# Attention and a Mamba block on one Trainium2 core: dt projected from high and low parts in one pass, and the maxima split before their transposes

## The chip, the cores and the metric

The kernel runs on one core of a Trainium2 chip. A core has five engines that run side by side and wait for each other by semaphores: TensorE (PE, matmuls, writes PSUM), VectorE (DVE), ScalarE (ACT), GpSimd (POOL) and SyncE (SP, which here only issues DMAs). The metric is the device time of one execution in microseconds; lower is better. All times of the profile are microseconds unless they are marked ns.

## The reference

The input x is (4, 128, 64, 64): four images of 128 channels and 4096 tokens. Two layers follow one another.

```python
# layer 0: attention over the 4096 tokens of an image, 4 heads of 32
Q, K, V = (split_heads(x_flat @ Wn + bn) for n in "qkv")
attn = softmax(Q @ K.T * 32**-0.5)                 # 4096 x 4096 per head
y = (attn @ V) @ Wo + bo + x_flat
x = (y - mean(y)) / sqrt(var(y) + 1e-5) * gamma + beta
# layer 1: three terms are summed
spatial  = conv3x3(x, conv_spatial_w) + conv_spatial_b
spectral = irfft2(conv_spectral_w @ [real, imag](rfft2(x)) + conv_spectral_b)
xi, z = split(in_proj_w @ x)                       # 256 + 256 rows
xs = silu(causal_conv1d(xi, 4 taps))
x_dbl = x_proj_w @ xs                              # 8 + 16 + 16 rows: dt's rank, B, C
dt = softplus(dt_proj_w @ x_dbl[:8] + dt_proj_b)   # 256 rows
h = exp(dt * A) * h + dt * B * xs                  # scan over the tokens, 16 states
out = spatial + spectral + out_proj_w @ ((h . C + D * xs) * silu(z))
```

## The kernel before

All tensors are float32 in memory. Some tiles are of the type float32r; the code splits a value into a high part that such a tile holds and the low rest, and multiplies both.

The tokens are cut into 32 chunks of 512 (8 per image). Attention runs over 64 halves H (a chunk's 512 queries and a pair of heads), each in 32 steps, one step per 128 keys. One outer loop runs over the steps t and writes the work of all stages side by side, by hand (`tc.manual_schedule()`); each engine works its instructions off in the order in which they are written. A step holds, in this order:

- `scores_for_exp(H, m)` (lines 475 to 492): six PE matmuls into the PSUM tile s (tag s2), the last two of which add minus the row's maximum as `sel` x `MX[H]`; then ACT takes exp into e.
- `scores_for_max` (427 to 446), for half H + 1 and seven steps ahead: four PE matmuls into the other s (tag s1), of which DVE takes maxima into part.
- pieces of the scan of an earlier chunk (`scan_state`, `scan_decay`, `scan_input_term`): dA on ACT, hs on DVE, db, hs and acc on POOL, and the load of B and C rows spread over partitions (bc) by SP.
- a turn of the plan, which runs jobs.
- `times_values` for the step before: two PE matmuls po with e.

Jobs are generators in a `Plan` (100 to 152). At each `yield` a job names what it needs next: "P", "D" or "A" are places on PE, DVE or ACT in this step, "B" one of two spare PSUM banks. In attention an odd step has two places of each kind, an even step one place on ACT alone; before and after attention each step has four of each. A job whose needs aren't met waits for a later step; jobs of low rank go first. `plan.release(bank, n)` gives the bank back n steps later.

The jobs that matter here are these.

- `maxima(H)` (448 to 471) starts seven steps ahead of half H, with rank 0. It takes a bank, reduces part to mx (128 x 8: 4 tiles of 128 queries x 2 heads) on DVE, copies each value over 64 columns into wide with four POOL copies (line 455), transposes the four tiles on PE into pm (462), and makes MX: ACT writes minus the high part to mhi (469), and DVE adds the low part on those rows for which `minus_lo` is set (470). MX has the high part in rows 0 to 31 of a head's 64 and the low part in rows 32 to 63; `sel` picks one row of each kind. Of these steps only the bank is asked for; the places of DVE, PE and ACT aren't.
- `scan_bc(c)` (707 to 721) multiplies xs by x_proj (pd, 40 rows: 8 of dt, 32 of B and C), lets ACT copy pd to xd, stores the 32 rows to bcd by an SP DMA, and starts two `scan_dt`.
- `scan_dt(c, hf, xd)` (723 to 761) multiplies the 8 rows by dt_proj, with both in float32 (pdt, line 726), for 128 of the 256 rows of dt; then follow the steps of softplus on ACT, DVE and POOL.
- `gate(c)` and `convolve(c)` compete with these for places (pz at line 769, pf at lines 903 and 908).

The weights are loaded at the start by DMAs that ACT issues (190 to 241). For the last two chunks, after attention has ended, the scan's sum is made on PE (acc, line 852).

Of the kernel before, what the change touches and what calls it, by code (L numbers as in the profile page):

```python
# [9 lines left out]
F32 = mybir.dt.float32  # L10
F32R = mybir.dt.float32r
AF = mybir.ActivationFunctionType
ALU = mybir.AluOpType
# [4 lines left out]
P = 128  # L18
W = 64
HEADS = 4  # L20
HD = P // HEADS
PAIRS = HEADS // 2
HS = P // 2
L = 512
RPC = L // W
TPC = L // P
DI = 256
NH = DI // P
NS = 16
DTR = 8  # L30
# [14 lines left out]

K_ID, K_HIL, K_G = 0, P, 2 * P
K_LO = K_G + W
K_SEL = K_LO + 1
NCONST = K_SEL + P


def _constants():

    w = np.arange(W)
    k = np.arange(1, W // 2)
    sin = np.sin(2 * np.pi * np.outer(w, k) / W).sum(1) * 2 / W
    hil = sin[(w[:, None] - w[None, :]) % W]
    c = np.zeros((P, NCONST), np.float64)
    c[:, K_ID : K_ID + P] = np.eye(P)  # L70
    for r in range(2):
        s = slice(r * W, (r + 1) * W)
        c[s, K_HIL + r * W : K_HIL + (r + 1) * W] = hil.T
    c[:, K_G : K_G + W] = -sin
    for j in range(2):
        c[j * HS + HD : (j + 1) * HS, K_LO] = 1.0
        c[j * HS, K_SEL : K_SEL + P] = 1.0
        c[j * HS + HD, K_SEL : K_SEL + P] = 1.0
    return c.astype(np.float32)


# [74 lines left out]
def attention_then_conv_mamba(  # L156
# [17 lines left out]
    nc = tc.nc  # L174
    ctx.enter_context(tc.manual_schedule())
    B, C, N = x.shape
# [6 lines left out]
    const = ctx.enter_context(tc.tile_pool(name="const", bufs=1))  # L183
    att = ctx.enter_context(tc.tile_pool(name="att", bufs=2))
    loc = ctx.enter_context(tc.tile_pool(name="loc", bufs=2))
# [9 lines left out]
    for h in range(HEADS):  # L195
        k, j = divmod(h, 2)
# [3 lines left out]
    for h in range(HEADS):  # L200
        k, j = divmod(h, 2)
        c = COL["bk"] + k
# [8 lines left out]
    for h in range(HEADS):  # L211
        k, j = divmod(h, 2)
        c = COL["bq"] + h
# [17 lines left out]
    nc.scalar.dma_start(cw, conv_w)  # L231
    inw = const.tile([P, 2 * DI], F32, name="inw")
    nc.scalar.dma_start(inw, in_w)
    xpw = const.tile([P, NH, DTR + 2 * NS], F32, name="xpw")
    nc.scalar.dma_start(xpw, xp_w.rearrange("(h p) r -> p h r", p=P))
    dtw = const.tile([DTR, DI], F32, name="dtw")
    nc.scalar.dma_start(dtw, dt_w)
    outw = const.tile([P, NH, P], F32, name="outw")
    nc.scalar.dma_start(outw, out_w.rearrange("(h p) o -> p h o", p=P))
    spw = loc.tile([P, 2, 2 * P], F32, tag="sgz", name="spw", bufs=1)  # L240
# [2 lines left out]
    def col(name, k=0):  # L243
        return vec[:, COL[name] + k : COL[name] + k + 1]

    in_lo = cst[:, K_LO : K_LO + 1]
    ident = cst[:, K_ID : K_ID + P]
    hilbert = cst[:, K_HIL : K_HIL + P]
    minus_lo = const.tile([P, 1], F32, name="minus_lo")
    sel = const.tile([P, P], F32R, name="sel")  # L250
    ones = const.tile([P, 1], F32, name="ones")
    nc.vector.memset(ones, 1.0)
# [9 lines left out]

    def constants_of_attention():
        yield ""
        nc.vector.tensor_scalar(minus_lo, in_lo, -1.0, None, ALU.mult)
        nc.vector.tensor_copy(sel, sel_f)

    def constants_of_the_rest():


        yield ""
        half = loc.tile([P, 2, 2 * P], F32, tag="sg1", name="half", bufs=1)
        nc.vector.tensor_scalar(half, spw, 0.5, None, ALU.mult)
        rr, ir = half[:, 0, :P], half[:, 0, P:]
        ri, ii = half[:, 1, :P], half[:, 1, P:]
        yield ""
        g_id = loc.tile([P, P], F32, tag="ob", name="g_id", bufs=1)
        nc.gpsimd.tensor_tensor(g_id, rr, ii, ALU.add)
        nc.gpsimd.tensor_tensor(cw[:, 4, :], cw[:, 4, :], g_id, ALU.add)
        nc.gpsimd.tensor_tensor(g_flip, rr, ii, ALU.subtract)  # L280
        nc.gpsimd.tensor_tensor(g_hil, ri, ir, ALU.subtract)
        nc.gpsimd.tensor_tensor(g_fliphil, ri, ir, ALU.add)
        yield ""
        nc.vector.tensor_scalar(sbias, cst[:, K_G : K_G + W], col("spec_bi"), None, ALU.mult)
        nc.vector.tensor_tensor(sbias[:, 0:1], sbias[:, 0:1], col("spec_br"), ALU.add)

        nc.scalar.activation(negA, vec[:, COL["A_log"] : COL["A_log"] + NH * NS], AF.Exp)
        yield ""
        nc.vector.tensor_scalar(negA, negA, -1.0, None, ALU.mult)


        bank = yield "PB"
        pb = bank_tile(bank, [P, 1], "pb")
        nc.tensor.matmul(pb, Wo, bvc, start=True, stop=True)
        yield "D"
        plan.release(bank, 2)
        nc.vector.tensor_tensor(bo, pb, col("bo"), ALU.add)
# [5 lines left out]
        [const.tile([P, L], F32R, name=f"K_{k}_{i}") for i in range(NCH)] for k in range(PAIRS)  # L303
    ]
    VA = [const.tile([P, TPC, HEADS, HD + 1], F32, name=f"V_{i}") for i in range(NCH)]
    state = const.tile([P, NH * NS], F32, name="state")
    carry = const.tile([P, NH, TAPS - 1], F32, name="carry")

# [5 lines left out]
    def bank_tile(bank, shape, name):  # L314
        return psum.tile(shape, F32, tag=f"m{bank}", name=name)
# [66 lines left out]
    QT, MX = {}, {}  # L382
# [64 lines left out]

    def maxima(H):

        bank = yield "B"  # L450
        mx = att.tile([P, TPC, 2], F32, tag="mx", name=f"mx_{H}")
        nc.vector.tensor_reduce(mx, part.pop(H), AX.X, ALU.max)  # L452
        wide = att.tile([P, TPC, 2, HS], F32, tag="wide", name=f"wide_{H}", bufs=1)
        for t in range(TPC):
            nc.gpsimd.tensor_copy(  # L455
                wide[:, t], mx[:, t].unsqueeze(2).to_broadcast([P, 2, HS])
            )
        for _ in range(3):
            yield ""
        pm = bank_tile(bank, [P, L], f"pm_{H}")  # L460
        for t in range(TPC):
            nc.tensor.transpose(
                pm[:, t * P : (t + 1) * P], wide[:, t].rearrange("p j d -> p (j d)"), ident
            )
        yield ""
        plan.release(bank, 2)
        mhi = att.tile([P, L], F32R, tag="th", name=f"mhi_{H}", bufs=1)
        mm = att.tile([P, L], F32R, tag="MX", name=f"MX_{H}")
        nc.scalar.activation(mhi, pm, AF.Copy, scale=-1.0)
        nc.vector.scalar_tensor_tensor(mm, mhi, minus_lo, pm, ALU.mult, ALU.subtract)  # L470
        MX[H] = mm

    es, po, oz = {}, {}, {}

# [232 lines left out]
    def scan_bc(c):  # L707

        bank = yield "PB"
        pd = bank_tile(bank, [DTR + 2 * NS, L], f"pd_{c}")  # L710
        for hf in range(NH):
            nc.tensor.matmul(pd, xpw[:, hf, :], xss[c][hf], start=hf == 0, stop=hf == NH - 1)
        yield "A"
        plan.release(bank)
        xd = loc.tile([DTR + 2 * NS, L], F32, tag="xd", name=f"xd_{c}", bufs=1)
        nc.scalar.activation(xd, pd, AF.Copy)
        yield ""
        bcds[c] = dram.tile([2 * NS, L], F32, tag="bc_d", name=f"bcd_{c}")
        nc.sync.dma_start(bcds[c], xd[DTR:, :])
        for hf in range(NH):  # L720
            plan.now(1, scan_dt(c, hf, xd))

    def scan_dt(c, hf, xd):
        bank = yield "PB"
        pdt = bank_tile(bank, [P, L], f"pdt_{c}_{hf}")
        nc.tensor.matmul(
            pdt, dtw[:, hf * P : (hf + 1) * P], xd[:DTR, :], start=True, stop=True
        )


        yield "A"
# [417 lines left out]
```

## Time and profile before

| | before |
|---|---|
| median of 3 runs | 6135.8 us (6135.27 to 6138.95) |
| the profiled execution: time, span | 6136.61 us, 6134.7 us |
| mean granted TensorE clock | 0.986 |
| busy: PE, DVE, ACT, POOL | 96%, 70%, 58%, 74% |
| pdt (line 726): records, mean ns | 128, 639 |
| wide (line 455): copies, busy | 256, 63.1 us |
| MX (line 470): operations, mean ns | 64, 746 |
| mhi (469) and xd (716): operations, mean ns | 64, 589 and 32, 577 |

Busy time is the sum of an engine's instructions over the span. PEld is the load of TensorE's weights, which overlaps PE's matmuls. Records of matmuls overlap each other too, so the mean length of a record is longer than the distance from one start to the next. A float32 product shows as two records, a float32r product as one. In the lines of groups there stand the line of the kernel, the engine, the operation, output<-inputs, shapes and count; then busy us and the mean ns of one; then the engine's idle time just before, with what ended most of it.

### The profile page before, as it was taken

What the parts mean: (1) busy time and instruction counts of PE and PEld (TensorE: products, weight loads), DVE (VectorE), ACT (ScalarE), POOL (GpSimd) and SP (SyncE); (2) the same over time, 40 slices, a digit from 0 to 9 for tenths busy, and PEclk for the clock granted to TensorE, in tenths of its full rate; (3) what the DMA queues carried; (4) which work ended last, traced back from release to release, by engine and by line L of the source; (5) the groups of instructions that cost most, each with busy time, mean ns of one, the idle gap of its engine ahead of it and who ended that gap; (6) DMA issues with size and microseconds to landing.
All of it is one profiled execution on the core that took longest, in us unless ns stands there. A gap on an engine that the chain in (4) does not pass through costs nothing. (4 is left out here: it accounts for less than half of the span.)

```text
span 6134.7 us, 82692 instructions
## 1 busy us (share of the span) xinstructions
PE 5914.9 (96%) x31434; PEld 2454.4 (40%) x31434; DVE 4291.6 (70%) x4404; ACT 3557.2 (58%) x4794; POOL 4534.8 (74%) x4785
## 2 busy tenths in 40 slices
PE   5999999999999999999999999999999999999966
PEld 2444444444444444444444444444444444444321
DVE  4556776777776777777767777677777677777647
ACT  1455666665666665666665666666565566566643
POOL 0006888778887777888877888877888787788877
PEclk7999999999999999999999999999999999999988
DMA  4012222224322222222332322222432222222222
GB/s 126 23 35 57 75 65 73 72 69 110 89 78 74 72 70 71 73 66 84 102 89 72 74 75 65 73 72 68 111 82 75 69 65 63 65 66 69 67 82 82
DMA packets 265503, 455.21 MB, mean 74 GB/s; under 512 B 45577, under 2 KB 47121, under 8 KB 265105
## 3 DMA queue, kind: packets, MB, share of 16 engines
q1 hardware_dynamic: 261584, 448.11, 26.9%
q8 instruction: 246, 4.03, 0.3%
q10 hardware_dynamic: 3520, 1.82, 0.1%
q14 instruction: 153, 1.25, 0.1%
HBM read 375.63 MB, written 65.80 MB: 72 GB/s over the span
## 5 line engine op out<-in xcount | busy, mean ns | idle before, releaser
L446 DVE TENSOR_REDUCE part<-s 128x2 f32<-128x1024 f32 x2048 | 2497.4, 1220 | 1527.0 <-PE s L439 1526.5
L491 ACT ACTIVATE e<-s 128x1024 f32<-128x1024 f32 x2048 | 2095.3, 1023 | 2203.1 <-PE s L483 2195.7
L503 PE MATMUL po<-e,V 128*33 128x512 f32 x8192 | 2158.6, 605 | 0.7
L483 PE MATMUL s<-Q,K 64*128 64x512 f32 x8192 | 1504.0, 445 | 7.1 <-ACT e L491 3.8
L439 PE MATMUL s<-K,Q 64*128 64x512 f32 x8192 | 1314.6, 398 | 31.5 <-DVE part L446 28.5
L839 POOL TENSOR_TENSOR hs<-hs,bc 128x512 f32<-128x512 f32 x952 | 1215.7, 1277 | 174.0 <-DVE hs L829 105.4
L483 PEld LDWEIGHTS s<-Q,K 64*128 64x128 f32 x8192 | 610.9, 185 | 1727.9 <-ACT e L491 1175.1
L818 POOL TENSOR_TENSOR db<-u,bc 128x512 f32<-128x512 f32 x948 | 1215.4, 1282 | 0.0
L858 POOL TENSOR_TENSOR acc<-acc,hs 128x512 f32<-128x512 f32 x900 | 1150.8, 1279 | 70.6
L829 DVE TENSOR_TENSOR_SCAN hs<-dA,state,db 128x512 f32<-128x512 f32 x832 | 1060.2, 1274 | 106.9 <-ACT dA L813 53.1
L439 PEld LDWEIGHTS s<-K,Q 64*128 64x128 f32 x8192 | 762.0, 185 | 255.2 <-DVE part L446 77.1
L483 PE MATMUL s<-MX,sel 64*128 64x512 f32 x4096 | 813.4, 394 | 25.9 <-DVE MX L470 25.9
L813 ACT ACTIVATE dA<-dt,negA 128x512 f32<-128x512 f32 x1024 | 703.1, 687 | 137.3 <-DVE hs L829 76.1
L838 POOL COPY state<-hs 128x1 f32<-128x1 f32 x864 | 159.9, 185 | 818.1 <-DVE hs L829 818.1
L503 PEld LDWEIGHTS po<-e,V 128*33 128x33 f32 x8192 | 299.8, 109 | 908.4 <-issue 894.1
L483 PEld LDWEIGHTS s<-MX,sel 64*128 64x128 f32 x4096 | 384.0, 184 | 129.2 <-DVE MX L470 38.6
L903 PE MATMUL pf<-xp,cw 128*128 128x512 f32 x576 | 288.5, 620 | 0.0
L455 POOL COPY wide<-mx 128x128 f32<-128x128 f32 x256 | 63.1, 290 | 202.5 <-DVE mx L452 202.5
L829 DVE TENSOR_TENSOR_SCAN hs<-dA,zero,db 128x512 f32<-128x512 f32 x128 | 163.0, 1274 | 1.5 <-POOL db L818 1.2
L852 PE MATMUL acc<-V,cst 128*128 128x512 f32 x128 | 92.4, 823 | 71.6 <-POOL V L839 71.2
L903 PEld LDWEIGHTS pf<-xp,cw 128*128 128x128 f32 x576 | 96.7, 188 | 135.4 <-issue 135.2
L701 POOL TENSOR_TENSOR xs<-xs,sg_x 128x512 f32<-128x512 f32 x64 | 82.4, 1287 | 59.1 <-ACT sg_x L625 59.1
(141 smaller groups left out, 3551.4 us busy)
## 6 DMA issues: line engine op xcount, KB each, us to landing
bc<-bcd SPq DMA_DIRECT2D x487, 512.0 KB
Q<-qd SPq DMA_DIRECT2D x256, 128.0 KB
K<-kd SPq DMA_DIRECT2D x64, 256.0 KB
K<-bcd SPq DMA_DIRECT2D x42, 256.0 KB
vd<-vst SPq DMA_DIRECT2D x32, 264.0 KB
V<-vd SPq DMA_DIRECT2D x32, 264.0 KB
xq<-in_x SPq DMA_DIRECT2D x32, 256.0 KB
xk<-in_x SPq DMA_DIRECT2D x32, 256.0 KB
```

The source lines that it names most:

```text
L439: nc.tensor.matmul(sc[:, j, :], QT[H][rows[j], n, t * P : (t + 1) * P], KK[k][m][rows[j], :], start=n == 0, stop=n == 1,)
L446: nc.vector.tensor_reduce(part[H][:, t, :, m], sc, AX.X, ALU.max)
L483: nc.tensor.matmul(s[:, j, :], sel[rows[j], :] if n == 2 else KK[k][i][rows[j], t * P : (t + 1) * P], mov[rows[j], :], start=n == 0, stop= ...
L491: nc.scalar.activation(e, s, AF.Exp)
L503: nc.tensor.matmul(po[H][used[j], :], VA[i][:, t, 2 * k + j, :], e[:, j, :], start=m == 0, stop=m == NT - 1,)
L813: nc.scalar.activation(dA[c, v], dts[c][hf], AF.Exp, scale=negA[:, k : k + 1])
L818: engine.tensor_tensor(db[c, v], us[c][hf], bcs[c, n][0], ALU.mult)
L829: nc.vector.tensor_tensor_scan(hs, dA.pop((c, v)), db.pop((c, v)), state[:, k : k + 1] if c % NCH else zero, ALU.mult, ALU.add,)
L838: nc.gpsimd.tensor_copy(state[:, k : k + 1], hs[:, L - 1 :])
L839: nc.gpsimd.tensor_tensor(hs, hs, bcs[c, n][1], ALU.mult)
L858: nc.gpsimd.tensor_tensor(accs[c, hf], accs[c, hf], hs, ALU.add)
L903: nc.tensor.matmul(pf, cw[:, k, :], xps[c][:, dy : dy + RPC, dx : dx + W], start=k == 0, stop=False)
```

## The change

The dt product. The x_proj weights of dt are laid down four times side by side in xpw, and the dt_proj weights four times one under the other in dtw, by nine DMAs in the place of two. pd then has 64 rows, of which the first 32 are four copies of dt's 8. ACT writes them to x4 as float32r, which keeps the high part, and one DVE operation takes the high part off again in the last two copies, so that x4 holds high, high, low, low. dtw is treated in the same way once, at the start, to high, low, high, low. One float32r product over 32 rows then gives the sum of all four products. xd holds B and C alone.

The maxima. wide becomes a constant tile of zeros. DVE takes the high part of minus mx, copies it to column 0 of each head's 64, and writes the low part to column 32; all this on 128 x 8 values. The transposes on PE stay, and ACT copies their result to MX. The job now asks for a place on DVE, then for a place on PE and a bank, then for a place on ACT.

```diff
--- before.py
+++ after.py
@@ -45,7 +45,7 @@
 
 K_ID, K_HIL, K_G = 0, P, 2 * P
 K_LO = K_G + W
-K_SEL = K_LO + 1
+K_SEL = K_LO + 2
 NCONST = K_SEL + P
 
 
@@ -73,9 +73,11 @@
         c[s, K_HIL + r * W : K_HIL + (r + 1) * W] = hil.T
     c[:, K_G : K_G + W] = -sin
     for j in range(2):
-        c[j * HS + HD : (j + 1) * HS, K_LO] = 1.0
         c[j * HS, K_SEL : K_SEL + P] = 1.0
         c[j * HS + HD, K_SEL : K_SEL + P] = 1.0
+    c[2 * DTR : 4 * DTR, K_LO] = -1.0
+    for j in range(2):
+        c[(2 * j + 1) * DTR : (2 * j + 2) * DTR, K_LO + 1] = -1.0
     return c.astype(np.float32)
 
 
@@ -231,10 +233,15 @@
     nc.scalar.dma_start(cw, conv_w)
     inw = const.tile([P, 2 * DI], F32, name="inw")
     nc.scalar.dma_start(inw, in_w)
-    xpw = const.tile([P, NH, DTR + 2 * NS], F32, name="xpw")
-    nc.scalar.dma_start(xpw, xp_w.rearrange("(h p) r -> p h r", p=P))
-    dtw = const.tile([DTR, DI], F32, name="dtw")
-    nc.scalar.dma_start(dtw, dt_w)
+
+    xpw = const.tile([P, NH, 4 * DTR + 2 * NS], F32, name="xpw")
+    xp_v = xp_w.rearrange("(h p) r -> p h r", p=P)
+    dtw = const.tile([4 * DTR, DI], F32R, name="dtw")
+    dtw_f = loc.tile([4 * DTR, DI], F32, tag="zg0", name="dtw_f", bufs=1)
+    for k in range(4):
+        nc.scalar.dma_start(xpw[:, :, k * DTR : (k + 1) * DTR], xp_v[:, :, :DTR])
+        nc.scalar.dma_start(dtw_f[k * DTR : (k + 1) * DTR, :], dt_w)
+    nc.scalar.dma_start(xpw[:, :, 4 * DTR :], xp_v[:, :, DTR:])
     outw = const.tile([P, NH, P], F32, name="outw")
     nc.scalar.dma_start(outw, out_w.rearrange("(h p) o -> p h o", p=P))
     spw = loc.tile([P, 2, 2 * P], F32, tag="sgz", name="spw", bufs=1)
@@ -243,10 +250,9 @@
     def col(name, k=0):
         return vec[:, COL[name] + k : COL[name] + k + 1]
 
-    in_lo = cst[:, K_LO : K_LO + 1]
+    less_x, less_w = (cst[:, K_LO + k : K_LO + k + 1] for k in range(2))
     ident = cst[:, K_ID : K_ID + P]
     hilbert = cst[:, K_HIL : K_HIL + P]
-    minus_lo = const.tile([P, 1], F32, name="minus_lo")
     sel = const.tile([P, P], F32R, name="sel")
     ones = const.tile([P, 1], F32, name="ones")
     nc.vector.memset(ones, 1.0)
@@ -262,7 +268,6 @@
 
     def constants_of_attention():
         yield ""
-        nc.vector.tensor_scalar(minus_lo, in_lo, -1.0, None, ALU.mult)
         nc.vector.tensor_copy(sel, sel_f)
 
     def constants_of_the_rest():
@@ -283,6 +288,9 @@
         yield ""
         nc.vector.tensor_scalar(sbias, cst[:, K_G : K_G + W], col("spec_bi"), None, ALU.mult)
         nc.vector.tensor_tensor(sbias[:, 0:1], sbias[:, 0:1], col("spec_br"), ALU.add)
+        high = loc.tile([4 * DTR, DI], F32R, tag="zg1", name="dtw_high", bufs=1)
+        nc.vector.tensor_copy(high, dtw_f)
+        nc.vector.scalar_tensor_tensor(dtw, high, less_w[: 4 * DTR], dtw_f, ALU.mult, ALU.add)
 
         nc.scalar.activation(negA, vec[:, COL["A_log"] : COL["A_log"] + NH * NS], AF.Exp)
         yield ""
@@ -303,6 +311,9 @@
         [const.tile([P, L], F32R, name=f"K_{k}_{i}") for i in range(NCH)] for k in range(PAIRS)
     ]
     VA = [const.tile([P, TPC, HEADS, HD + 1], F32, name=f"V_{i}") for i in range(NCH)]
+
+    wide = const.tile([P, TPC, 2, HS], F32, name="wide")
+    nc.gpsimd.memset(wide, 0.0)
     state = const.tile([P, NH * NS], F32, name="state")
     carry = const.tile([P, NH, TAPS - 1], F32, name="carry")
 
@@ -447,28 +458,24 @@
 
     def maxima(H):
 
-        bank = yield "B"
+        yield "D"
         mx = att.tile([P, TPC, 2], F32, tag="mx", name=f"mx_{H}")
         nc.vector.tensor_reduce(mx, part.pop(H), AX.X, ALU.max)
-        wide = att.tile([P, TPC, 2, HS], F32, tag="wide", name=f"wide_{H}", bufs=1)
-        for t in range(TPC):
-            nc.gpsimd.tensor_copy(
-                wide[:, t], mx[:, t].unsqueeze(2).to_broadcast([P, 2, HS])
-            )
-        for _ in range(3):
-            yield ""
+        hi = att.tile([P, TPC, 2], F32R, tag="mhi", name=f"mhi_{H}")
+        nc.vector.tensor_scalar(hi, mx, -1.0, None, ALU.mult)
+        nc.vector.tensor_copy(wide[:, :, :, 0], hi)
+        nc.vector.scalar_tensor_tensor(wide[:, :, :, HD], mx, -1.0, hi, ALU.mult, ALU.subtract)
+        yield ""
+        bank = yield "PB"
         pm = bank_tile(bank, [P, L], f"pm_{H}")
         for t in range(TPC):
             nc.tensor.transpose(
                 pm[:, t * P : (t + 1) * P], wide[:, t].rearrange("p j d -> p (j d)"), ident
             )
-        yield ""
-        plan.release(bank, 2)
-        mhi = att.tile([P, L], F32R, tag="th", name=f"mhi_{H}", bufs=1)
-        mm = att.tile([P, L], F32R, tag="MX", name=f"MX_{H}")
-        nc.scalar.activation(mhi, pm, AF.Copy, scale=-1.0)
-        nc.vector.scalar_tensor_tensor(mm, mhi, minus_lo, pm, ALU.mult, ALU.subtract)
-        MX[H] = mm
+        yield "A"
+        plan.release(bank)
+        MX[H] = att.tile([P, L], F32R, tag="MX", name=f"MX_{H}")
+        nc.scalar.activation(MX[H], pm, AF.Copy)
 
     es, po, oz = {}, {}, {}
 
@@ -707,25 +714,28 @@
     def scan_bc(c):
 
         bank = yield "PB"
-        pd = bank_tile(bank, [DTR + 2 * NS, L], f"pd_{c}")
+        rank = 4 * DTR
+        pd = bank_tile(bank, [rank + 2 * NS, L], f"pd_{c}")
         for hf in range(NH):
             nc.tensor.matmul(pd, xpw[:, hf, :], xss[c][hf], start=hf == 0, stop=hf == NH - 1)
-        yield "A"
-        plan.release(bank)
-        xd = loc.tile([DTR + 2 * NS, L], F32, tag="xd", name=f"xd_{c}", bufs=1)
-        nc.scalar.activation(xd, pd, AF.Copy)
+        yield "DA"
+        plan.release(bank, 2)
+        xd = loc.tile([rank + 2 * NS, L], F32, tag="xd", name=f"xd_{c}", bufs=1)
+        x4 = loc.tile([rank, L], F32R, tag="dtr", name=f"dtr_{c}", bufs=1)
+        nc.scalar.activation(xd[rank:, :], pd[rank:, :], AF.Copy)
+        nc.scalar.activation(x4, pd[:rank, :], AF.Copy)
+        nc.vector.scalar_tensor_tensor(x4, x4, less_x[:rank], pd[:rank, :], ALU.mult, ALU.add)
         yield ""
         bcds[c] = dram.tile([2 * NS, L], F32, tag="bc_d", name=f"bcd_{c}")
-        nc.sync.dma_start(bcds[c], xd[DTR:, :])
+        nc.sync.dma_start(bcds[c], xd[rank:, :])
         for hf in range(NH):
-            plan.now(1, scan_dt(c, hf, xd))
-
-    def scan_dt(c, hf, xd):
+            plan.now(1, scan_dt(c, hf, x4))
+
+    def scan_dt(c, hf, x4):
+
         bank = yield "PB"
         pdt = bank_tile(bank, [P, L], f"pdt_{c}_{hf}")
-        nc.tensor.matmul(
-            pdt, dtw[:, hf * P : (hf + 1) * P], xd[:DTR, :], start=True, stop=True
-        )
+        nc.tensor.matmul(pdt, dtw[:, hf * P : (hf + 1) * P], x4, start=True, stop=True)
 
 
         yield "A"
```

## The prediction

> **What bounds the kernel now.** I read the busy line, the windows by stage, the list of TensorE's waits and then the timeline of single steps. The chain of work that ended last covers only the last few microseconds and says nothing here.
>
> ```profile
> PE 5914.9 (96%) x31434; PEld 2454.4 (40%) x31434; DVE 4291.6 (70%) x4404; ACT 3557.2 (58%) x4794; POOL 4534.8 (74%) x4785
> ```
>
> TensorE (PE) is busy for 96% of the span. The windows (length, then busy time of PE, PEld, DVE, ACT, POOL, then granted clock) show where the other 4% lies:
>
> ```profile
> 0.00:130.00 130.00, 62.57 (x252) 30.92 (x252) 53.36 (x59) 13.76 (x21) 5.02 (x23) 0.74 0.47 145
> 3000.00:4000.00 1000.00, 991.84 (x5380) 413.97 (x5378) 727.66 (x751) 611.35 (x826) 812.23 (x847) 1.00 0.28 74
> 5880.00:5930.00 50.00, 17.19 (x60) 5.77 (x59) 29.25 (x39) 24.41 (x39) 45.36 (x48) 0.69 0.21 57
> ```
>
> Between 130 and 5880 us PE is busy 99% at full clock; the start (130 us) and the tail (250 us) are bound elsewhere, the tail mostly by POOL and DVE. Its waits in the steady part are small (us in total, times, longest):
>
> ```profile
> PE s L439 <- DVE part L446: 28.5, 51, 1.5
> PE s L483 <- DVE MX L470: 25.9, 29, 1.1
> PE s L483 <- ACT e L491: 3.8, 13, 1.0
> ```
>
> The first is mostly in the start (1.9 us per 1000 us later); the second is spread over the whole of attention. So in the steady part a microsecond taken off PE's queue, or off the wait for MX, is a microsecond of the end. The Trainium skill, "Perfetto Trace Analysis", section Identifying the Most-Contended Engine, warns that matmul busy time is no measure of the distance to the peak; I use only the absence of gaps and the distance between starts. The timeline gives the price of a step and of a dt product (PE alone; the scores' rows between are left out):
>
> ```profile
> 1508.02 1.12 PE L726 MATMUL pdt<-xd,dtw 8*128 8x512 f32 x2
> 1509.07 1.13 PE L903 MATMUL pf<-xp,cw 128*128 128x512 f32 x2
> 1510.13 1.05 PE L503 MATMUL po<-e,V 128*33 128x512 f32 x4
> 1512.49 1.05 PE L503 MATMUL po<-e,V 128*33 128x512 f32 x4
> ```
>
> A bare step lasts 1512.49 - 1510.13 = 2.36 us. A dt product (two records, float32) adds 1.05 us before the next matmul starts. Neither ACT (about 1.02 for e) nor DVE (1.22 for the maxima) fills such a step.
>
> The wait for MX (all engines, other rows left out):
>
> ```profile
> 3079.31 0.59 ACT L469 ACTIVATE mhi<-pm 128x512 fp32r<-128x512 f32 x1
> 3079.93 0.75 DVE L470 SCALAR_TENSOR_TENSOR MX<-mhi,minus_lo,pm 128x512 fp32r<-128x512 f32 x1 [0.46 <-ACT mhi L469]
> ...
> 3080.73 0.50 PE L483 MATMUL s<-MX,sel 64*128 64x512 f32 x2 [0.88 <-DVE MX L470]
> ```
>
> In 29 halves, every second one from the first late one on, the transposes stand only two steps before the first use of MX; ACT (behind e and dA) and then DVE make MX one after the other, and PE stands for 0.9 us.
>
> **What the skill says.** "TensorE: Matmul & The Clock Gate", LDWEIGHTS: a weight load costs by its columns, not by its rows. The trace agrees: 183 ns for dtw's 8 x 128, about 188 ns for 128 x 128. So 32 rows cost PE nothing over 8. Same page, Back-to-back issue gap: a matmul of N=512 follows another after 518 cycles, 216 ns. The trace agrees as to one pass: the second product of a pf group starts 0.85 us after the first, (1.91 - 1.06), four passes of 0.21; and a pair of sel products on float32r takes 0.24 us (3000.77 to 3001.01), one pass. "DMA: Bandwidth & Descriptors", Specifications: below 512 B a transfer loses rate; the copied x_proj pieces are 32 B runs. No row of before shows the price.
>
> **The dt product.** 64 products; 62 lie in the steady part (chunk 31's two are in the tail). Before: 1.05 us each. After: one float32r pass of 0.21 to 0.24 us, plus what is paid on entering a group (1.05 - 0.85 = 0.2). The order of the changed kernel puts both halves of a chunk in one step. Lower bound of the pair: 0.2 + 2 x 0.21 = 0.62, less if the entry also shrinks (0.48); upper: both pay an entry and an unhidden load of 0.18, 0.85. I take 0.65: 2.10 - 0.65 = 1.45 us per pair, x 31 = **-45 us** (39 to 50).
> What feeds it: pd gets 64 output columns instead of 40 (same passes; its load of 116 ns grows by some 20, under 1 us in all). ACT writes xd and x4 separately: one more op of 0.58 x 32 = 18.5 us; DVE gets one operation of up to 0.75 x 32 = 24 us. In the step of these, ACT has e 1.02 + dA 0.69 + 2 x 0.58 = 2.87 us; in 30 of 32 chunks that same step holds a gate product pz on PE, so it lasts 2.36 + 1.06 = 3.42, and DVE's operation ends before the next scores are there. The product itself stands two steps (over 5 us) behind x4. SP's store of bcd waits for xd alone and stands at most three DMAs later in SP's queue; three bc buffers cover that. I put stalls at +2 us (0 to +10; the cover is gone where pz moves away: then up to 0.5 us x 32).
>
> **The maxima.** PE keeps four 128 x 128 transposes per half: 0. POOL loses 256 copies, 63.1 us, none on the path in the steady part. DVE loses 64 x 0.75 for MX and gets three operations on 8 elements; the nearest rows are 0.13 (one element) and 0.17 (32), so 64 x about 0.5 = 32: a gain of 16 us on an engine with slack. ACT's pass over pm stays (0.59). All four DVE operations now stand together, two steps ahead of the transposes; queued behind them is the next maximum of part, delayed by 0.5 us, which a 2.36 us step with 1.22 (or 2.5 with a scan, recovered in the next step) absorbs. In the order of the changed kernel the transposes of the late halves stand one step earlier than before, and MX is made by ACT alone in the step after, directly behind e: ready about 2.6 us after that step's start, needed over 5 us after it. So the 0.9 us wait goes: **-26 us** (-20 to -26; late next would be DVE's maximum, which has 2.5 us less to do there).
>
> **Start.** ACT issues nine DMAs where two stood, and its first real operation stands behind them:
>
> ```profile
> 13.54 0.45 ACTq L235 DMA_DIRECT2D xpw<-in_xp_w  x1
> 14.03 0.60 ACTq L237 DMA_DIRECT2D dtw<-in_dt_w  x1
> ...
> 15.10 0.47 ACTq L241 DMA_DIRECT2D spw<-in_spec_w  x1
> 15.69 0.69 ACT L402 ACTIVATE qhi<-pq,bq 128x512 fp32r<-128x512 f32 x1 [13.67 <-PE pk L335]
> ```
>
> qhi starts right after the last issue although pq is there by 13.7. Seven more at 0.47 = +3.3 us, handed on through kd, the loads of xk and all the start; small pieces may add to DMA time. I take **+4** (0, if the later loads wait for DMA anyway, to +8). The memset of wide on POOL, the two operations on dtw on DVE (0.2 to 0.4 each; DVE loses MX's 0.75 there) are hidden: POOL idles 22 us, and the maxima wait for PE at half clock.
>
> **Tail.** Chunk 30's dt work stands some four POOL operations earlier, so more of it falls under attention; chunk 31's products are shorter on a PE that ACT waits for (7.5 us before dt). Against that 0.58 ACT and 0.75 DVE. **-3** (-8 to +3).
>
> Sum: -45 + 2 - 26 + 4 - 3 = -68 us. The profiled execution took 6136.6 us (span 6134.7, 1.9 around it), 0.8 above the median of 6135.8. 6136.6 - 68 - 0.8 = **6068 us**, 1.1% less.
>
> **Rivals.**
> (1) The MX wait comes back in another form: A now needs a place, so ACT's pass could stand behind other jobs. Against it: in the order it stands behind e alone. Then only dt counts: 6136 - 45 + 3 = 6094.
> (2) The dt gain turns into a wait for ACT: the s bank is single, e ends about 0.27 us before the next scores start, so shorter steps could expose ACT. For it: that margin; against: the step of the two products holds e, dA and one sigmoid pass, 2.33 us, in 3.0. If two thirds are lost: 6068 + 30 = 6098. The same if float32r needs more than one pass over 32 rows, which the sel rows speak against.
> (3) Slower: the transposes wait for DVE. Place: PE, at pm, in each of 64 halves; before, POOL's copies stood there with more steps between. From the start of the step with the four operations DVE is done after about 1.4 + 1.2 + 0.7 = 3.3 us, pm comes at 4.7 + 1.4 = 6.1: slack 2.8. To lose 80 us (the 68 and 12 to be measured) DVE must be 2.8 + 80/64 = 4.0 us behind in every half: 6148 and more. PE's longest wait for DVE's maximum is 1.5 us, so this is unlikely.
>
> **How the numbers follow.** The main case 0.79, (1) 0.08, (2) 0.07, (3) 0.03, and 0.03 that the losses eat the gain to within 0.2% (12 us, about what a measurement can tell from no change). Faster 0.94, same 0.03, slower 0.03. Bounds of the main case: -50 - 26 - 8 + 0 = -84 if all falls well, -39 - 20 + 8 + 10 + 3 = -38 if all falls ill; all ends at once are unlikely, and the range reaches up toward (1) and (2): 6054 to 6092.
>
> **What would show it.** Right: pdt has 64 records with about 0.3 us between starts, and PE's busy time falls by some 40 to 50; the wait of s for MX is gone from PE's list; PE stays at 99% from 130 us on; qhi starts near 19 us; POOL some 63 us less busy. Wrong: PE waits of over 10 us for e, part, wide or dtr, a window share of PE clearly under 99%, or pdt at two records.

## The result and the profile after

| | before | after |
|---|---|---|
| median (4 runs each, side by side) | 6137.2 us | 6060.7 us (6057.8 to 6064.1) |
| profiled execution: time, span | 6136.6, 6134.7 us | 6062.5, 6060.8 us |
| busy: PE, DVE, ACT, POOL | 5914.9, 4291.6, 3557.2, 4534.8 us | 5849.3, 4360.3, 3585.5, 4488.8 us |
| start / attention / tail | 128.3 / 5759.5 / 246.9 us | 131.7 / 5683.6 / 245.5 us |

The ratio is 0.9876 (95% interval 0.9862 to 0.9891): the changed kernel is 1.2% faster. Attention is here the time from the first to the last start of a `sel` product (output s, input MX) on PE; start and tail are what lies before and behind. Such a split is read from one profiled execution of each kernel. It is much sharper than the total: two pairs of kernels further down whose attention is the same (the changed kernel and e6_start, e7_release and e9_best) agree in it to 0.1 us.

The page of the changed kernel, its windows (same columns as before) and its two waits that count in attention:

```profile
PE 5849.3 (97%) x31370; PEld 2443.2 (40%) x31370; DVE 4360.3 (72%) x4565; ACT 3585.5 (59%) x4826; POOL 4488.8 (74%) x4530
```

```profile
0.00:130.00 130.00, 63.59 (x240) 30.24 (x240) 52.17 (x57) 12.85 (x20) 4.55 (x21) 0.74 0.47 145
3000.00:4000.00 1000.00, 993.46 (x5440) 417.45 (x5440) 749.47 (x787) 618.81 (x834) 803.49 (x805) 1.00 0.29 75
```

```profile
PE s L450 <- DVE part L457: 28.9, 57, 1.4
...
PE s L490 <- ACT e L498: 10.2, 44, 1.4
```

PE is still the bound. The wait for MX (25.9 us) is gone from the list. The total of the wait for DVE's maximum looks unchanged, 28.9 against 28.5 us, but the wait for ACT's e went from 3.8 us in 13 places to 10.2 us in 44. The busy share of PE in a window (99%) shows none of this: 1000 us at 99.3% leave room for several such waits.

The timeline at the two dt products (PE alone, the scores between left out):

```profile
2943.64 1.05 PE L510 MATMUL po<-e,V 128*33 128x512 f32 x4
...
2945.98 0.72 PE L738 MATMUL pdt<-dtr,dtw 32*128 32x512 f32 x2
2946.64 1.05 PE L510 MATMUL po<-e,V 128*33 128x512 f32 x4
...
2948.98 1.05 PE L510 MATMUL po<-e,V 128*33 128x512 f32 x4
```

From pdt to po is 0.66 us for the pair, where one single product added 1.05 us before. The step of the pair lasts 2946.64 - 2943.64 = 3.00 us, the next, bare one (a step without a job on PE) 2.34.

The groups (line, engine, operation, shapes and count; busy us, mean ns; idle before) have a surprise:

```profile
L738 PE MATMUL pdt<-dtr,dtw 32*128 32x512 f32 x64 | 23.8, 445 | 0.0
...
L467 DVE SCALAR_TENSOR_TENSOR wide<-mx,mhi 128x8 f32<-128x8 f32 x64 | 67.0, 1046 | 0.0
...
L465 DVE TENSOR_SCALAR mhi<-mx 128x8 fp32r<-128x8 f32 x64 | 21.6, 338 | 2.2
L466 DVE COPY wide<-mhi 128x8 f32<-128x8 f32 x64 | 20.0, 313 | 2.3
```

The low part of the maxima, an operation on 128 x 8 values, takes 1046 ns in the mean: nearly as long as DVE's maximum over 128 x 1024. With the other two (338 and 313 ns) and the reduction to mx (0.22 us) the maxima cost DVE 1.9 us per half, not the 0.7 of the prediction. The timeline of DVE and POOL at one of them shows what runs beside it:

```profile
2862.99 1.27 POOL L849 TENSOR_TENSOR hs<-hs,bc 128x512 f32<-128x512 f32 x1
...
2863.81 0.48 DVE L465 TENSOR_SCALAR mhi<-mx 128x8 fp32r<-128x8 f32 x1
...
2864.34 1.30 POOL L868 TENSOR_TENSOR acc<-acc,hs 128x512 f32<-128x512 f32 x1
2864.40 1.27 DVE L467 SCALAR_TENSOR_TENSOR wide<-mx,mhi 128x8 f32<-128x8 f32 x1
```

L465 ends (2864.29) when POOL's L849 ends (2864.26); L467 ends (2865.67) when POOL's L868 ends (2865.64). So it is throughout: 53 of the 64 operations of L467 last over 0.25 us, and all 53 end within 0.08 us of the end of a POOL operation; the shortest takes 158 ns. The Trainium skill, "GPSIMD Engine Reference", section Specifications, states that POOL shares its SBUF interfaces with VectorE, with contention where a DVE instruction has two SBUF inputs or runs in a two-port mode. The trace agrees for L467, which has two. That POOL holds these operations is read from ends that coincide; no run took POOL's work away from beside them.

At the start, ScalarE's queue and its first operation:

```profile
18.37 0.48 ACTq L248 DMA_DIRECT2D spw<-in_spec_w  x1
18.96 0.69 ACT L413 ACTIVATE qhi<-pq,bq 128x512 fp32r<-128x512 f32 x1 [16.94 <-DMA xpw<-in_xp_w]
```

qhi starts right after the last issue, 3.3 us later than before (15.69).

### The profile page after: what moved, and what is told of

It reads as the page before. It is cut to its first block, busy times and chain, and to the rows that moved or that the text cites. A ratio compares the mean times of both kernels' runs of the same rounds, so it can differ in the third digit from the quotient of the medians.

```text
span 6060.8 us, 82716 instructions
## 1 busy us (share of the span) xinstructions
PE 5849.3 (97%) x31370; PEld 2443.2 (40%) x31370; DVE 4360.3 (72%) x4565; ACT 3585.5 (59%) x4826; POOL 4488.8 (74%) x4530
## 5 line engine op out<-in xcount | busy, mean ns | idle before, releaser
L510 PE MATMUL po<-e,V 128*33 128x512 f32 x8192 | 2180.9, 605 | 2.4 <-DVE oz L521 0.3
L490 PE MATMUL s<-Q,K 64*128 64x512 f32 x8192 | 1500.6, 444 | 13.5 <-ACT e L498 10.2
L450 PE MATMUL s<-K,Q 64*128 64x512 f32 x8192 | 1314.7, 399 | 38.0 <-DVE part L457 28.9
L849 POOL TENSOR_TENSOR hs<-hs,bc 128x512 f32<-128x512 f32 x952 | 1215.9, 1277 | 170.7 <-DVE hs L839 101.4
L868 POOL TENSOR_TENSOR acc<-acc,hs 128x512 f32<-128x512 f32 x900 | 1154.7, 1283 | 70.6
L839 DVE TENSOR_TENSOR_SCAN hs<-dA,state,db 128x512 f32<-128x512 f32 x832 | 1060.6, 1275 | 52.6 <-ACT dA L823 37.9
L823 ACT ACTIVATE dA<-dt,negA 128x512 f32<-128x512 f32 x1024 | 703.4, 687 | 113.4 <-DVE V L839 54.7
L554 POOL TENSOR_TENSOR op<-op,rz 128x512 f32<-128x512 f32 x32 | 40.9, 1278 | 178.5 <-DMA rz<-rd 175.6
L839 DVE TENSOR_TENSOR_SCAN hs<-dA,zero,db 128x512 f32<-128x512 f32 x128 | 163.2, 1275 | 1.0 <-POOL db L828 0.7
```

The source lines that it names most:

```text
L450: nc.tensor.matmul(sc[:, j, :], QT[H][rows[j], n, t * P : (t + 1) * P], KK[k][m][rows[j], :], start=n == 0, stop=n == 1,)
L490: nc.tensor.matmul(s[:, j, :], sel[rows[j], :] if n == 2 else KK[k][i][rows[j], t * P : (t + 1) * P], mov[rows[j], :], start=n == 0, stop= ...
L510: nc.tensor.matmul(po[H][used[j], :], VA[i][:, t, 2 * k + j, :], e[:, j, :], start=m == 0, stop=m == NT - 1,)
L823: nc.scalar.activation(dA[c, v], dts[c][hf], AF.Exp, scale=negA[:, k : k + 1])
L839: nc.vector.tensor_tensor_scan(hs, dA.pop((c, v)), db.pop((c, v)), state[:, k : k + 1] if c % NCH else zero, ALU.mult, ALU.add,)
L849: nc.gpsimd.tensor_tensor(hs, hs, bcs[c, n][1], ALU.mult)
```

## The experiments

All times are medians; kernels on one chip share the runs of the kernel before (6136.2 to 6137.4). Four edits carry names here: the **dt part**; the maxima's **form** (old: POOL copies, ACT then DVE make MX; new: columns split on DVE, ACT makes MX), their **place** (old: bank first, transposes three steps later; new: places asked for, transposes when PE has one), and the plan's **bank** (given back after one step or two).

### The dt part alone

e1_dt is the changed kernel with the maxima of before; the only difference is that minus the high part is written into MX itself and DVE adds to it in place.

```diff
-        nc.scalar.activation(mhi, pm, AF.Copy, scale=-1.0)
-        nc.vector.scalar_tensor_tensor(mm, mhi, minus_lo, pm, ALU.mult, ALU.subtract)
+        nc.scalar.activation(mm, pm, AF.Copy, scale=-1.0)
+        nc.vector.scalar_tensor_tensor(mm, mm, minus_lo, pm, ALU.mult, ALU.subtract)
```

> The dt part alone; the maxima keep their old form and place (ACT's high part goes into MX itself, DVE finishes it there). Theory: the two parts add up. pdt has 64 records; the two products of a chunk stand 10 steps apart in this order, so each pays its entry: some 0.45 us each in place of 1.05, 0.6 x 62 = -37 us; the wait of s for MX stays at about 26 us in some 29 halves; the start is 3.3 us later as in the changed kernel: about 6103 us (6096 to 6108). Rival, that most of the gain comes from the new packing of jobs into steps and not from the passes: within 15 us of the kernel before.

Measured: 6108.1 us, ratio 0.9952 (0.9937 to 0.9967); attention 5729.8 us, 29.7 less than before. The list of PE's waits has the old line with the old size:

```profile
PE s L493 <- DVE MX L480: 25.7, 29, 1.1
```

With the maxima at their old place the two products of a chunk still stand in different steps. Each then adds 0.43 us (from its start to that of the next product), so the pair costs 0.86 and not 0.66. By that price 2 x (1.05 - 0.43) x 31 = 38.4 us should have been gained. What is missing lies in one bare step of 28 chunks, the one behind a single dt product at the change of halves: these steps are longer by 9.0 us in all (median 2.79 us, before 2.35). Here is one (all other rows left out):

```profile
3353.27 0.50 PE L741 MATMUL pdt<-dtr,dtw 32*128 32x512 f32 x1
3353.38 1.28 DVE L842 TENSOR_TENSOR_SCAN hs<-dA,state,db 128x512 f32<-128x512 f32 x1
...
3354.58 1.20 DVE L457 TENSOR_REDUCE part<-s 128x2 f32<-128x1024 f32 x1
...
3355.83 0.73 PE L450 MATMUL s<-K,Q 64*128 64x512 f32 x4 [0.18 <-DVE part L457]
```

PE reaches the next scores sooner, but DVE, with a scan and the maximum to do, does not, and PE waits for it in all 28.

### The maxima's part alone

The kernel before with the changed kernel's `maxima` and its constant tile:

```diff
+    wide = const.tile([P, TPC, 2, HS], F32, name="wide")
+    nc.gpsimd.memset(wide, 0.0)
...
+        yield "D"
...
+        bank = yield "PB"
...
+        yield "A"
```

> The maxima alone; dt stays a float32 product over 8 rows, with two DMAs at the start. Theory: the wait for MX (25.9 us) goes and nothing comes in its place: about 6110 us (6104 to 6114), pdt at 128 records, PE's list of waits without MX. Rival, that DVE's small operations (1.9 us per half in the changed kernel, of which 1.0 for the low part) cost PE something: then PE's wait for part rises by 5 to 15 us and the time is 6115 to 6125.

Measured: 6102.2 us, ratio 0.9943 (0.9928 to 0.9958); attention 5726.3, 33.2 less. The MX wait is gone, and the waits for part and e have grown:

```profile
PE s L441 <- DVE part L448: 31.5, 60, 1.4
...
PE s L481 <- ACT e L489: 10.6, 45, 1.4
```

That is 8 us better than expected, more than the MX wait itself was worth, so the maxima's part does something else as well. And the two parts alone add up to 62.9 us of attention where both together give 75.9.

### The same order with the product in float32

The changed kernel with dtw, and likewise the tiles high and x4, in float32:

```diff
-    dtw = const.tile([4 * DTR, DI], F32R, name="dtw")
+    dtw = const.tile([4 * DTR, DI], F32, name="dtw")
...
```

> The changed kernel with xpw, dtw and x4 as they are, but dtw, its high part and x4 are float32 tiles, so the product over 32 rows is a float32 one, at the same place in the same order (the low parts are then zero). Theory: the passes alone make the dt gain: the pair of products goes from 0.66 us back to about 2.0 us, x 31 = +42 us over the changed kernel: 6103 us (6097 to 6108). Rival, that the order makes it: within 10 us of the changed kernel, 6061 to 6071.

Measured: 6102.7 us, ratio 0.9944 (0.9927 to 0.9960), 42 us above the changed kernel; attention 5722.1, 38.5 more. The products now have twice the records:

```profile
L738 PE MATMUL pdt<-dtr,dtw 32*128 32x512 f32 x128 | 63.8, 615 | 0.0
```

The step of the pair lasts 4.24 instead of 2.99 us; 1.25 x 31 = 38.8 us. The passes alone are worth that, in this order.

### The old form at the new place

The changed kernel, its yields in `maxima` kept, with the operations of before in between:

```diff
+            nc.gpsimd.tensor_copy(wide[:, t], mx[:, t].unsqueeze(2).to_broadcast([P, 2, HS]))
...
         yield "A"
-        plan.release(bank)
-        nc.scalar.activation(MX[H], pm, AF.Copy)
+        plan.release(bank, 2)
+        nc.scalar.activation(mm, pm, AF.Copy, scale=-1.0)
+        nc.vector.scalar_tensor_tensor(mm, mm, minus_lo, pm, ALU.mult, ALU.subtract)
```

> The changed kernel with the maxima in their old form (four POOL copies into wide, then ACT, then DVE) at the new place in the order (transposes two steps behind DVE's maximum, one step earlier in the late halves). Theory, that the place removes the wait for MX: MX's wait is gone, since ACT and DVE have two steps. But POOL's copies stand behind db in its queue and came 5.4 us after mx in one half of the kernel before, while the transposes come some 2.8 us after it: PE then waits for wide at pm, 1 to 3 us in some 29 halves, +30 to +80 us: 6090 to 6140. Rival, that POOL is early enough: no wait at pm, within 5 us of the changed kernel.

Measured: 6048.8 us, ratio 0.9856 (0.9841 to 0.9871); attention 5670.1, 13.5 **less** than the changed kernel. PE's waits:

```profile
PE s L450 <- DVE part L457: 14.1, 24, 1.3
...
PE s L493 <- ACT e L501: 3.5, 13, 0.7
PE pm L473 <- POOL wide L466: 2.2, 3, 0.8
```

So the theory fell: at the new place the old form waits neither for MX nor, but for 2.2 us, for POOL. Its rival, a time within 5 us of the changed kernel, missed as well. I took the 12 us by which it beats the changed kernel for the price of the slow operations on DVE. But e4_oldform differs in one more thing: its bank comes back a step later, because DVE still reads pm. That had to be parted.

### The new form at the old place

The columns are split as in the changed kernel; the yields around that and around the transposes are those of before:

```diff
-        yield "D"
+        bank = yield "B"
...
-        yield ""
-        bank = yield "PB"
+        for _ in range(3):
+            yield ""
...
-        yield "A"
-        plan.release(bank)
+        yield ""
+        plan.release(bank, 2)
```

> The maxima's new form (columns split before the transposes, one ScalarE copy makes MX) at the old place in the order (bank claimed first, transposes three steps later); the dt product as in the changed kernel. Theory A, the form alone is enough: the chain from transposes to MX loses VectorE's 0.72 us and one hand-over, the MX wait of 25.7 us goes, and the time is that of e1_dt less some 25: 6083 us (6078 to 6092). Theory B, only the new place removes the wait: 6103 to 6110 us, with an MX wait of 20 us or more on PE.

Measured: 6086.4 us, ratio 0.9919 (0.9904 to 0.9934); attention 5709.1, 20.7 less than e1_dt. As to the wait theory A holds: without DVE's operation in the chain no more than one wait of 0.4 us for MX is left. The form alone removes it, as the place alone did in e4_oldform. At the old place the wait for the maximum is now longer than in e1_dt (27.7 us):

```profile
PE s L450 <- DVE part L457: 35.9, 77, 1.4
```

The small operations are in its way (timeline, other rows left out):

```profile
3596.66 1.26 DVE L467 SCALAR_TENSOR_TENSOR wide<-mx,mhi 128x8 f32<-128x8 f32 x1
...
3597.83 1.21 DVE L457 TENSOR_REDUCE part<-s 128x2 f32<-128x1024 f32 x1
...
3599.10 0.74 PE L450 MATMUL s<-K,Q 64*128 64x512 f32 x4 [0.66 <-DVE part L457]
```

The order on PE is that of e1_dt in every step, so the two can be compared step by step. The 29 bare steps that waited for MX are 22.8 us shorter in all, but 20 steps with a projection, right behind the small operations, are 12.8 us longer. What makes the sum come out near 20 all the same is a third part, told under "The sum". So the expected time was met in part by luck.

### One number: the bank after two steps

```diff
-        plan.release(bank)
+        plan.release(bank, 2)
```

> The changed kernel with one number edited: the maxima's bank is given back two steps after the transposes' copy instead of one. On PE this moves the first of the two input projections of each late half one step later, beside no other change to the attention's order, and gives the order of e4_oldform; the new form of the maxima stays. Theory A, the 12 us between e4_oldform and the changed kernel come from the two projections falling into one step, after which VectorE is behind in the next short steps: the time falls to 6049 us (6046 to 6053), and VectorE's part wait falls from 28.9 us to about 14. Theory B, they come from the four small VectorE operations of 1.9 us per half: the time stays at 6058 to 6062.

Measured: **6032.7 us**, ratio 0.9831 (0.9817 to 0.9846), 28 us less than the changed kernel; attention 5656.0. The direction is theory A's and the size more than twice it: theory A took e4_oldform's time for its measure, and at the same order the new form has turned out faster (see "The sum"). PE's waits:

```profile
PE s L450 <- DVE part L457: 16.3, 29, 1.4
...
PE s L490 <- ACT e L498: 3.5, 13, 0.7
```

12.6 us less for the maximum and 6.7 less for e: 19.3 of the 27.6 us of attention. In nearly all of attention PE's order differs from the changed kernel's in a single group of matmuls per chunk: in the changed kernel both input projections of a chunk (pi, line 683) stand in one step; with the later bank there is none free for the second, and it goes to the next step with places, two steps on (the expectation had it as the first, and one step). What follows in the changed kernel (timeline; all other rows left out):

```profile
2877.86 1.23 DVE L457 TENSOR_REDUCE part<-s 128x2 f32<-128x1024 f32 x1 [3.03 <-PE s L450]
...
2879.47 0.69 DVE L521 COPY oz<-po 33x512 f32<-33x512 f32 x1 [0.39 <-ACT oz L520]
...
2880.20 1.28 DVE L839 TENSOR_TENSOR_SCAN hs<-dA,state,db 128x512 f32<-128x512 f32 x1
...
2881.39 1.20 DVE L457 TENSOR_REDUCE part<-s 128x2 f32<-128x1024 f32 x1
...
2882.65 0.73 PE L450 MATMUL s<-K,Q 64*128 64x512 f32 x4 [0.47 <-DVE part L457]
...
2884.53 0.74 PE L490 MATMUL s<-Q,K 64*128 64x512 f32 x4 [0.17 <-ACT e L498]
```

In the long step of both projections DVE idles for 3.03 us. Two steps later, at the change of halves, DVE has the copy of po, which waits for ACT's copy of the same tile, then a scan, then the maximum: 2881.39 + 1.20 - 2879.09 (the end of the maximum before) = 3.5 us in a step of 2.34, and PE waits 0.47 us; then it waits for e, which ACT makes late behind the copies of the second projection. The bare step that holds these two waits lasts 3.32 us in the median, against 2.34 in e7_release, and over 30 chunks this makes 28.0 us, all of the difference. With the projections in two steps, one of them lies beside this work and covers it.

### The low part twice

```diff
         nc.vector.scalar_tensor_tensor(wide[:, :, :, HD], mx, -1.0, hi, ALU.mult, ALU.subtract)
+        nc.vector.scalar_tensor_tensor(wide[:, :, :, HD], mx, -1.0, hi, ALU.mult, ALU.subtract)
```

> e7_release with VectorE's low-part operation issued twice, the second writing the same values again: up to 1.27 us more on VectorE in each of 64 halves. Theory A, the small operations of the maxima lie in a long PE step and cost nothing there: 6031 to 6036 us, part wait within 3 us of e7_release's 16.3. Theory B, VectorE has no room at that place: each pushes the next reduction back and PE waits, up to 81 us more in all, and at least 10 us more: 6043 or above.

Measured: 6065.0 us, ratio 0.9884 (0.9870 to 0.9897), 32 us more than e7_release; attention 5687.9, 31.9 more. Theory B holds. The timeline, and the wait's total:

```profile
2868.55 1.24 DVE L468 SCALAR_TENSOR_TENSOR wide<-mx,mhi 128x8 f32<-128x8 f32 x1
...
2869.71 1.21 DVE L457 TENSOR_REDUCE part<-s 128x2 f32<-128x1024 f32 x1
...
2870.98 0.73 PE L450 MATMUL s<-K,Q 64*128 64x512 f32 x4 [0.32 <-DVE part L457]
```

```profile
PE s L450 <- DVE part L457: 39.3, 79, 1.6
```

The second operation too ends with a POOL operation in all 52 long cases. A step with the transposes lasts 3.50 us in place of 2.92: of 1.2 us more on DVE some 0.6 reach PE, in 52 steps 30 us. So in e7_release the first one, long as it is, just fits, with some 0.6 us to spare in the mean.

### Fewer issues ahead of qhi

One load fills the last of the four places in xpw and three POOL copies the others; SP issues the four loads of dtw_f, later.

```diff
-    for k in range(4):
-        nc.scalar.dma_start(xpw[:, :, k * DTR : (k + 1) * DTR], xp_v[:, :, :DTR])
-        nc.scalar.dma_start(dtw_f[k * DTR : (k + 1) * DTR, :], dt_w)
-    nc.scalar.dma_start(xpw[:, :, 4 * DTR :], xp_v[:, :, DTR:])
+    nc.scalar.dma_start(xpw[:, :, 3 * DTR :], xp_v)
...
```

> The changed kernel with its first loads thinned: one load of the projection weights on ScalarE's queue and three GpSimd copies that repeat them, and the four loads of dt's weights issued later by SyncE; eight DMA issues fewer on ScalarE ahead of qhi. Theory: those issues are the 3.3 us by which qhi starts later (18.96 against 15.69 us), so qhi comes back to about 15 us and the time falls by 3 to 4 us, to about 6057. Rival: the first load that qhi waits for lands no earlier, or the start is bound by loads behind it: no change, 6060 to 6061.

Measured: 6058.3 us, ratio 0.9872 (0.9855 to 0.9888). qhi starts at 15.4 us instead of 19.0, the start stage is 2.3 us shorter (129.4), attention is the same (5683.7). The total's 2.5 us lie inside both intervals, and the start stage is itself unsteady: six kernels with the changed kernel's loads (e1, e3, e4, e5, e7, e10) had it between 128.8 and 132.2. The mechanism is seen at qhi; its worth in the end isn't separated.

### The later bank and the thinner start together

```diff
-    for k in range(4):
...
+    nc.scalar.dma_start(xpw[:, :, 3 * DTR :], xp_v)
...
-        plan.release(bank)
+        plan.release(bank, 2)
```

> The two edits that gained apart, together: e7_release's bank given back after two steps and e6_start's thinned first loads. If they add, 6032.7 less the 2.5 us of e6_start: 6030 us (6027 to 6033), with qhi at about 15.4 us. If the start's gain is lost further on (a later wait for the first loads of x), 6032 to 6034.

Measured: **6030.9 us** (6029.6 to 6034.5), ratio 0.9829 (0.9815 to 0.9842), attention 5656.1: the fastest version here, 0.5% below the changed kernel. Its lead over e7_release (1.8 us) isn't separated.

### The sum

Attention, by the distance between successive steps: a bare step (no job on PE) is compared with 2.355 us, and so are the steps with jobs. 2047 x 2.355 = 4820.7 us, and the two columns on the right make up the rest.

| kernel | dt | form | place | bank | attention | mean bare step | bare steps over | steps with jobs over |
|---|---|---|---|---|---|---|---|---|
| before | old | old | old | 2 | 5759.5 | 2.394 | 54.7 | 884.1 |
| e1_dt | new | old | old | 2 | 5729.8 | 2.399 | 60.5 | 848.6 |
| e5_newform | new | new | old | 2 | 5709.1 | 2.376 | 29.8 | 858.6 |
| e7_release | new | new | new | 2 | 5656.0 | 2.358 | 4.9 | 830.4 |
| after | new | new | new | 1 | 5683.6 | 2.380 | 36.4 | 826.5 |
| e4_oldform | new | old | new | 2 | 5670.1 | 2.364 | 12.7 | 836.7 |

From row to row: dt -29.7, form -20.7, place -53.1, bank +27.6; together -75.9.

One effect runs through these rows without being a wait. The median bare step lasts 2.356 or 2.357 us in the three kernels with the old form (before, e1_dt, e4_oldform) and 2.341 to 2.343 in the eight with the new one, at either place; the 2.36 and 2.34 us read from the timelines above are these. e4_oldform and e7_release have the same order on PE in all 2047 steps, and 13.1 of the 14.1 us between them come from steps that differ by 40 ns or less. Nearly all of it is in the scores for the maximum: from their start to the next product the median in bare steps is 567 ns with the old form and 558 with the new. The maxima's own operations run once in 32 steps, so PE isn't waiting for them there; why its scores are shorter no run shows. Between e1_dt and e5_newform such small differences make 14.2 of the 20.7 us.

## Why the prediction was right, and where it was not

The forecast was 6068 (6054 to 6092), faster; measured 6060.7. Its total is right, but what makes it up is in part something else.

How much each part is worth depends on the order in which the parts are added. By the table, dt gives 29.7 us of attention and the maxima's part 46.2. The other way round, the maxima's part alone (e2_max) gives 33.2, and dt on top of it 42.7, close to the 26 and the 43 (45 less 2) of the forecast. Seen this way the terms are nearly right; but the maxima's term is made of larger pieces, some gains and some losses, which the forecast did not price. That they nearly cancel is luck.

- **dt, -45 (39 to 50): right in mechanism and price.** The pair costs 0.66 us (0.65 forecast), one float32r pass for 32 rows and one entry for both. In the changed order the passes are worth 38.5 us (e3_f32), and the rest of the 45 is the entry shared by the pair. That sharing is a gift of the maxima's new place, and so is a step behind it in which DVE is not late: alone, in the old order, the dt part gave 29.7, 6 us less for the entries (0.86 - 0.66, 31 times) and 9.0 less for the wait for DVE.
- **Stalls that feed it, +2: nothing of it is seen in the changed order.** The wait for e did rise, as rival (2) feared, from 3.8 to 10.2 us. But e2_max, without the dt part, has 10.6, and e7_release, with it, 3.5. It comes with the two projections in one step, not with dt.
- **MX wait, -26: gone, as forecast.** The step named two reasons, ACT alone and one step more of lead. Each is enough alone (e5_newform, e4_oldform). What it missed is that removing a wait at one place leaves PE free to wait at the next (at the old place 22.8 us were gained in the steps that had waited, and 12.8 lost behind the small operations), and that the new form also makes the scores a little shorter, 13.1 us from e4_oldform to e7_release and 14.2 from e1_dt to e5_newform, which the forecast had at nothing ("PE keeps four 128 x 128 transposes"). Mean bare steps fell only from 2.394 to 2.380.
- **The place was not priced at all.** This is the step that failed: I used the changed order for where pdt and the transposes stand, and didn't ask which other jobs it moves. The place is worth 53 us of attention with the new form and 60 with the old. In the 60 the MX wait can be no more than 26; in the 53 it has no part, since the new form had already removed it. About half of the 53 lies in bare steps (29.8 to 4.9 us over), 14.6 of it in the 28 steps behind a single dt product, and about half in steps with jobs, more of which share a step; the wait for the maximum falls by 19.6 in all. I have no experiment that divides it further. And the bank that comes back a step sooner pairs the projections, which costs 27.6. With both unpriced, -69 in attention could end as -75.9 only because one went against the other.
- **DVE in the maxima, 0.5 us for the three small operations: mis-sized.** They take 1.7, each long one ending with a POOL operation; DVE got 68.7 us busier where some 8 had been forecast (24 of dt less 16 of the maxima). "A gain on an engine with slack" was a loss that fits into the slack of one place, and at the old place did not fit. The slack was mis-sized too: rival (3) gave the transposes 2.8 us, but what stands behind these operations first is the next maximum, and e10_twice shows it has only some 0.6 us in the mean. The rival's mechanism was near; it needed one more operation, not 4 us in every half.
- **Start, +4: +3.4, tail, -3: -1.4.** The cause at the start, the issues ahead of qhi, is seen as forecast; the size stays within what the start varies by.
- **Rival (1)**, only dt counts, is what e1_dt looks like in its waits, at 6108 instead of 6094: the entries that are not shared make 6 us of this, the step behind the first product 9. That step is the mechanism of **rival (2)**, a shorter step that exposes another engine, with DVE in the place of ACT.

- **The signs it had named.** pdt's 64 records, the end of the MX wait, PE at 99% and qhi at 19 us came as told. PE's busy time fell by 65.6 us and not by 40 to 50; e2_max, without the dt part, has 22.6 of it. POOL's fell by 46 and not by 63. And one sign of being wrong appeared, if barely: over 10 us of waiting for e.

Not settled: why the scores for the maximum are shorter with the new form. It is nearly all of the 14.1 us of attention by which e7_release beats e4_oldform, and it is spread over more than half of the steps, so it is not POOL's 2.2 us wait for wide, and the wait for the maximum is even 2.2 us longer in the new form.

## What to carry to other kernels

When a planner decides the order, price a change by the whole order that it produces: list every job that moved on the bound engine, also those that the diff doesn't touch, and ask for each bare step behind a long one whether the second engine can still finish in it. A resource that comes free a step earlier can cost more than it gives. When two kernels have the same order, compare them step by step: a gain of some ns in every step stands in no list of waits. And before a small operation is called cheap, look at what runs beside it on the engine that shares its memory ports, and in which step the next urgent operation of that queue is due.

## What was unexpected of the hardware

DVE's operation on 128 x 8 values with two SBUF operands lasts 158 ns at the shortest, but in 53 of 64 cases it goes on to the end of a POOL operation of 1.3 us and lasts up to 1275 ns (median of all 1266). The same holds for the one-operand operations around it, more rarely for the copy: L466 is long in 8 of 64 cases (174 ns to 1.42 us), and all 8 end with a POOL operation. In these runs the length of such an operation went with what POOL was doing, not with its own size.

Two kernels with the same order, shapes and types of matmuls can differ in the length of a step: between e4_oldform and e7_release the scores for the maximum go from 567 to 558 ns in the median bare step. The cause is open.
